# Layer 3's two store transfers issued by SP in place of ScalarE, placed between the loads of two steps

## The chip, the cores and the metric

The kernel runs on one core of a Trainium2 chip. A core has five engines that this text speaks of: TensorE (matrix products into PSUM), VectorE, ScalarE (activation functions), GpSimd, and SP, which here only issues transfers between the chip's main memory (DRAM) and on-chip memory (SBUF). Each engine works through its own list of instructions in order, and engines wait for one another by semaphores. The metric is the device time of one execution in microseconds (us), lower is better.

## The reference

The input is a float32 image tensor of 2 x 128 channels x 64 x 64. Four layers follow one another: layer 0 is a four-direction selective scan with layer norm and projections, layers 1 and 2 are spatial attention over 4096 positions, and layer 3, the one that is changed, is a short selective scan along the channels:

```python
seq = x.transpose(0, 2, 3, 1).reshape(B * H * W, TOKEN_NUM, D_MODEL)   # 8 tokens of 16
xz = seq @ in_proj_w.T;  xi, z = jnp.split(xz, 2, axis=-1)             # 32 inner channels
xs = jax.nn.silu(conv1d(xi))                                           # 4 taps, per channel
dt, Bm, Cm = jnp.split(xs @ x_proj_w.T, [1, 17], axis=-1)              # 16 states
dt = jax.nn.softplus(dt @ dt_proj_w.T + dt_proj_b)
h = exp(dt * A) * h + dt * Bm * xs                                     # 8 tokens in turn
y = (sum over states of h * Cm + xs * D) * silu(z)
out = y @ out_proj_w.T        # back to 128 channels; then group norm (4 groups), silu, + x
```

Every one of the 8192 pixels is a sequence of its own: its 128 channels are cut into 8 tokens of 16 channels. The recurrence over the tokens keeps 32 inner channels x 16 states per pixel.

## The kernel before, in words

In layer 3 a **chunk** is 512 pixels (T); there are 16 chunks, 8 for each of the two images. Within a chunk the 8 tokens are taken two at a time, so a chunk has four **steps** k = 0 to 3, and a step has two tokens, o = 0 and 1. The 128 partitions hold 4 state groups x 32 inner channels, and a tile of 4 x 512 elements per partition holds the other factor 4 of the states and the pixels. The arithmetic of a step uses four kinds of work:

- `spread(k)` (line 1232) loads the time step of two tokens from DRAM (`ddt`) into `dtr`, copied to the four partition groups: eight transfers of 64 KB, or four for k = 0. `da_(k)` (line 1273) is ScalarE's exponential of it, giving tile A.
- `load(k, o)` (line 1244) loads the 16 rows of B of one token from DRAM (`rows`) into a tile D, each row broadcast to 32 partitions: four transfers of 256 KB. A step has two such tiles, step 3 only one. There are six D buffers in turn, two `dtr` buffers.
- `db_` (line 1266) multiplies D, on VectorE and in two halves, by the time step times x (`rx`, from TensorE).
- The recurrence: `mul` (line 1283, GpSimd) multiplies A by the state before, `add` (line 1288, VectorE or GpSimd) adds that to D, which is then the new state. `hc_` (line 1306, VectorE) multiplies by C (`q`, from TensorE) and TensorE sums over the states into `y`.

`rows` and `ddt` are written once per chunk, one chunk ahead. `b_` makes B by a matrix product, ScalarE copies it from PSUM to SBUF (`bs`, line 1191), and the copy is stored to `rows` (line 1193). The time step `dt` is finished by GpSimd (`dt_add`, line 1217; `dtx_`, line 1220, makes dt times x), and is stored to `ddt` (line 1224). Both stores stand on ScalarE's list of instructions, all the loads on SP's.

The order of the instructions on each engine is written out by hand: the part runs under `manual_schedule`, and nothing is reordered. A loop over all steps s of all chunks has four groups g = 0 to 3 in a step. `PLAN` gives the recurrence of a group in letters: `m` is `mul` (on GpSimd), `v` and `g` are `add` on VectorE and GpSimd, `D` is `db_` for the step to come, `C` is `hc_` for the step before, `time` is `dt_add` and `dtx_`. For step 0, `PLAN` reads

```python
("m10 m11 C D", "C D time", "C v10 D", "g11 D C"),
```

and for step 1 `("m00 m01 C D v00", "C v01 D m10 m11", "v10 D", "g11 D")`. Other work is hung on a group by `more((k, g), ...)`, ahead of it (`at=first`) or behind it. The loads that go out in step s are those of step s + 2 (`n2`): in step 0 of a chunk the loads of its step 2, in step 2 those of the next chunk's step 0. The stores of the next chunk (`fut`) are in step 0: `b_` ahead of group 0, `put` behind group 2. The first chunk's own stores and loads stand ahead of the loop.

Each transfer signals its end on one of eight semaphores, which are given out in turn over the transfers of SP's and ScalarE's lists together, in an order set when the kernel is built. A transfer that gets a semaphore waits first until the transfer that had it before has landed.

Of the kernel before, what the change touches and what calls it, by code (L numbers as in the profile page):

```python
# [57 lines left out]
def conv_seq_kernel(ctx: ExitStack, tc: tile.TileContext, a: dict, out: bass.AP):  # L58
    nc = tc.nc
# [39 lines left out]
    with ExitStack() as c0:  # L99
# [9 lines left out]
        def wt(tag, bufs=None, shape=(P, 2, T)):  # L109
            return wk_.tile(list(shape), F32, tag=tag, name=tag, bufs=bufs)  # L110
# [386 lines left out]
        with tc.manual_schedule():  # L497
            c, c1 = chunks[:2]
# [234 lines left out]
    with ExitStack() as c1:  # L733
# [256 lines left out]
        def put(slot, *steps):  # L990
            for i, f in enumerate(steps):
                todo.setdefault(slot + i, []).append(f)

        def piece(slot, j, what, qd, later=0):

            steps = []

            def first():
                steps.extend(getattr(j, what)(qd))
                steps[0]()  # L1000

            n = 2 if j.layer == 2 else 7 if what == "value_piece" else 5
            put(slot, first, *[lambda i=i: steps[i]() for i in range(1, min(n, 5))])
            put(slot + 5 + later, *[lambda i=i: steps[i]() for i in range(5, n)])

        for n, j in enumerate(jobs):
            s0 = n * NG * UPG
            if n == 0:
                continue
            for g, what, qd in ((9, "key_piece", 0), (10, "value_piece", 0), (11, "key_piece", 1),  # L1010
                                (12, "value_piece", 1)):
                piece(s0 + (g - NG) * UPG + 5, j, what, qd)
            piece(s0 - UPG + 4, j, "key_piece", 2)
            piece(s0 - UPG + 9, j, "key_piece", 3)
            piece(s0 + 12, j, "value_piece", 2)
            piece(s0 + UPG + 2, j, "value_piece", 3)
            if jobs[n - 1].layer == 1:
                for ci in range(NCH):
                    c = Conv(jobs[n - 1].b, ci)
                    put(s0 + (1 + ci) * UPG + 11, lambda c=c: c.taps(0), lambda c=c: c.taps(1),  # L1020
                        lambda c=c: c.taps(2), c.end)
# [68 lines left out]
    with ExitStack() as c3:  # L1090
# [61 lines left out]
        class Chunk3:  # L1152
# [35 lines left out]
            def b_(self):  # L1188
                p = self.bc_(0)
                self.bs = wt("bs", (P, T), bufs=1)  # L1190
                nc.scalar.copy(self.bs, p)
                self.rows = dr.tile([P, T], F32, tag="rows", name="rows")
                nc.scalar.dma_start(self.rows, self.bs)

            def c_(self):
                self.pc = self.bc_(1)
# [24 lines left out]

            def put(self):
                self.ddt = dr.tile([P, 2, T], F32, tag="ddt", name="ddt")
                nc.scalar.dma_start(self.ddt, self.dt)

            def spread(self, k):

# [190 lines left out]
        with tc.manual_schedule():  # L1418
            mm(y, lhsT=ident, rhs=x[:, 0, 0:T], start=True, stop=True)
            c, c1 = chunks[:2]  # L1420
            for i in range(2):
                c.xs_(i)
            c.b_()
            for i in range(2):
                c.dt_(i)
            c.e_exp()
# [15 lines left out]
            for s in range(-1, len(steps) + 3):  # L1442
# [3 lines left out]
                fut = chunks[ci + 1] if s >= 0 and ci + 1 < len(chunks) else None  # L1446
# [8 lines left out]
                def more(key, *what, at=extra):  # L1455
                    at.setdefault(key, []).extend(what)

                if fut is not None:
                    more((0, 0), fut.b_, at=first)
                    more((0, 1), fut.c_, at=first)  # L1460
                    more((0, 2), fut.put, fut.cb_)
                if old is not None:
                    more((1, 0), lambda: old.yg_(1))
                    more((2, 1), old.xr_, at=first)
# [199 lines left out]
```

## Time and profile before

| | before |
|---|---|
| runs, us | 6688.31, 6689.05, 6681.28 (median 6688.31) |
| profiled execution, us | 6684.23 |
| its span, first to last instruction, us | 6682.4 |
| busy: TensorE, VectorE, ScalarE, GpSimd, us | 5857.7, 5536.6, 4477.6, 5404.5 |
| layer 3 (5640 to 6683): TensorE, VectorE, ScalarE, GpSimd, us | 846.61, 855.85, 473.99, 796.78 |
| granted TensorE clock, span and layer 3 | 0.863, 0.83 |
| store of rows, of ddt: issue on ScalarE's queue, us | 0.33, 0.33 |
| the same: issue to landing, us (median) | 2.0, 3.0 |
| load of D, of dtr: issue to landing, us (median) | 6.0, 3.0 |

The profile is of one execution. Engines are called PE (TensorE), PEld (its weight loads), DVE (VectorE), ACT (ScalarE), POOL (GpSimd) and SP; SPq and ACTq are the issues of transfers on an engine's list. A line of a list of waits reads: who waited, for what, the total in us, how many times, the longest. A line of the timeline reads: start and length in us, engine, line of the kernel, operation, output and inputs, count; in brackets the idle time of that engine just before it, and what ended that. What ended a wait is inferred from the semaphores.

### The profile page before, as it was taken

To read this page: it belongs to the slowest core of one execution; us is meant where nothing else is said; L and a number is where in the kernel's file an instruction comes from. 1 tells how busy PE (TensorE), PEld (TensorE's weight loads), DVE (VectorE), ACT (ScalarE), POOL (GpSimd) and SP (SyncE) were. 2 spreads that over 40 slices of the span, in tenths; PEclk is the share of its full clock that TensorE was granted. 3 is DMA by queue.
4 is the path that set the end of the run, shared out by engine and by line. 5 is a ranking of instruction groups with operands and counts; after the bars stand their busy time and mean duration, and the time that the engine had idled before them with its cause. 6 is when DMAs were issued, how large, how long until landed. Compare 5 with 4: busy or idle time off the path is not lost. (4 is left out here: it accounts for less than half of the span.)

```text
span 6682.4 us, 66184 instructions
## 1 busy us (share of the span) xinstructions
PE 5857.7 (88%) x19918; PEld 2766.3 (41%) x19918; DVE 5536.6 (83%) x4462; ACT 4477.6 (67%) x7740; POOL 5404.5 (81%) x2473
## 2 busy tenths in 40 slices
PE   8888888888888888888879999999999997888787
PEld 2222222222222222222228887787788885222221
DVE  7999999999999999999986665565566765788888
ACT  7887788877788777887766664455455554444443
POOL 6999999999999999999986665555556665788787
PEclk7888778877788778887779999999999998788888
DMA  6666666566656666665640000000000001766765
GB/s 182 145 155 157 156 149 150 147 150 152 151 143 146 154 154 148 154 149 146 146 106 5 4 4 1 1 1 1 1 1 1 1 1 26 198 160 163 187 162 138
DMA packets 400473, 700.59 MB, mean 105 GB/s; under 512 B 74089, under 2 KB 76530, under 8 KB 399730
## 3 DMA queue, kind: packets, MB, share of 16 engines
q1 hardware_dynamic: 394624, 681.74, 42.1%
q10 hardware_dynamic: 5490, 14.63, 0.6%
q8 instruction: 156, 2.56, 0.2%
q14 instruction: 203, 1.66, 0.1%
HBM read 584.80 MB, written 111.28 MB: 104 GB/s over the span
## 5 line engine op out<-in xcount | busy, mean ns | idle before, releaser
L384 POOL TENSOR_TENSOR dbu<-dus,bs 128x1024 f32<-128x1024 f32 x1024 | 2459.6, 2437 | 101.0 <-DVE h L428 86.5
L428 DVE TENSOR_TENSOR_SCAN h<-da,hst,dbu 128x1024 f32<-128x1024 f32 x896 | 2091.4, 2341 | 94.1 <-ACT dbu L412 88.8
L397 ACT ACTIVATE da<-dts,aneg 128x512 f32<-128x512 f32 (+1 forms) x2048 | 1410.2, 689 | 350.2 <-DVE h L428 312.1
L924 POOL TENSOR_TENSOR sum<-sum,sc 128x1024 f32<-128x1024 f32 x384 | 906.0, 2360 | 492.1 <-ACT sc L919 488.3
L886 ACT COPY sc<-s 128x512 f32<-128x512 f32 x1024 | 597.0, 584 | 859.7 <-PE s L881 745.8
L893 DVE TENSOR_TENSOR mx<-mx,s 128x512 f32<-128x512 f32 x896 | 609.4, 680 | 546.3 <-ACT sc L886 545.0
L881 PE MATMUL s<-q,k 128*128 128x256 f32 x4096 | 1051.8, 380 | 6.4 <-ACT q L838 3.0
L451 PE MATMUL y<-hc,cst 128*32 128x512 f32 x4096 | 881.8, 757 | 198.6 <-DVE hc L440 179.3
L936 PE MATMUL av<-sc,v 128*128 128x256 f32 x4096 | 1048.6, 379 | 2.5 <-ACT sc L919 2.5
L440 DVE TENSOR_TENSOR hc<-h,pc 128x1024 f32<-128x1024 f32 x704 | 842.1, 1196 | 10.7 <-PE y L451 8.6
L881 PEld LDWEIGHTS s<-q,k 128*128 128x128 f32 x4096 | 776.7, 190 | 140.5 <-issue 29.0
L936 PEld LDWEIGHTS av<-sc,v 128*128 128x128 f32 x4096 | 768.2, 190 | 102.9 <-ACT sc L919 3.9
L438 POOL TENSOR_TENSOR hc<-h,cs 128x1024 f32<-128x1024 f32 x320 | 761.2, 2379 | 1.1 <-issue 1.1
L417 PE MATMUL pc<-xd,sel 16*128 16x512 f32 x1024 | 707.9, 782 | 1.5 <-DVE hc L440 1.3
L1283 POOL TENSOR_TENSOR A<-A,D 128x1024 f32<-128x1024 f32 x224 | 526.8, 2370 | 194.1 <-DVE D L1288 146.4
L916 DVE TENSOR_TENSOR sc<-sc,pm 128x1024 f32<-128x1024 f32 x512 | 620.3, 1212 | 0.9 <-PE pm L912 0.9
L919 ACT ACTIVATE sc<-sc 128x1024 f32<-128x1024 f32 x512 | 542.0, 1059 | 8.6 <-DVE sc L916 8.1
L341 PE MATMUL misc<-xd,w_dt 9*128 9x512 f32 x504 | 371.6, 825 | 141.9 <-ACT x L480 78.3
L451 PEld LDWEIGHTS y<-hc,cst 128*32 128x32 f32 x4096 | 125.4, 120 | 855.7 <-DVE hc L440 419.2
L412 ACT ACTIVATE dbu<-hst,dbu,df 128x1 f32<-128x1 f32 x896 | 337.9, 377 | 81.6 <-POOL dbu L384 59.0
L1266 DVE TENSOR_TENSOR D<-D,rx 128x1024 f32<-128x1024 f32 x224 | 268.6, 1211 | 143.9 <-DMA D<-rows 120.3
L1300 PE MATMUL q<-xs,lc 32*128 32x512 f32 x896 | 301.0, 678 | 64.9 <-DVE A L1306 63.9
(263 smaller groups left out, 7561.9 us busy)
## 6 DMA issues: line engine op xcount, KB each, us to landing
dts<-ddt SPq DMA_DIRECT2D x512, 256.0 KB, 5.5
dus<-ddu SPq DMA_DIRECT2D x512, 256.0 KB, 5.0
D<-rows SPq DMA_DIRECT2D x448, 256.0 KB, 6.0
bs<-rows SPq DMA_DIRECT2D x1024, 64.0 KB, 4.9
cs<-rows SPq DMA_DIRECT2D x1024, 64.0 KB, 3.3
ddt<-dt SPq DMA_DIRECT2D x128, 256.0 KB, 2.0
ddu<-dtu SPq DMA_DIRECT2D x128, 256.0 KB, 4.0
dtr<-ddt SPq DMA_DIRECT2D x448, 64.0 KB, 3.0
```

Of the source, the lines that this page charges most:

```text
L384: nc.gpsimd.tensor_mul(t, self.dus[q], _bc(self.bs[g], 1, [P, 2, T]))
L397: act(t[:, i, sl], self.dts[q][:, i, sl], AF.Exp, scale=an[:, g, 2 * q + i : 2 * q + i + 1])
L417: mm(t, lhsT=sel[32:48, 4 * g : 4 * g + 4, :].rearrange("p n d -> p (n d)"), rhs=self.xd[32:48, :], start=True, stop=True)
L428: nc.vector.tensor_tensor_scan(ho, ai, bi, init, ALU.mult, ALU.add)
L438: nc.gpsimd.tensor_mul(t, self.h[u], _bc(self.cs[gq(u)[0]], 1, [P, 2, T]))
L440: nc.vector.tensor_mul(t, self.h[u], _bc(self.pc[u // 2], 1, [P, 2, T]))
L451: mm(self.y[q // 2][r : r + 32, :], lhsT=sum4, rhs=self.hc[u][:, i, :], start=False, stop=(u % 8 >= 6), skip_group_check=True)
L881: mm(p[:, o, :], lhsT=j.k[m // 8][:, m % 8 * P : m % 8 * P + P], rhs=self.q, start=True, stop=True)
L893: nc.vector.tensor_max(self.mx, self.s[0][:, 0:2, :] if u == 1 else self.mx, self.p[u])
L916: nc.vector.tensor_sub(s, s, _bc(self.pm[:, :], 1, [P, 4, NQ]))
L924: nc.gpsimd.tensor_add(self.sum, self.s[0] if w == 1 else self.sum, self.s[w])
L936: mm(self.av, lhsT=self.job.v[m // 8][:, m % 8, :], rhs=self.s[u // 2][:, m % 4, :], start=(m == 0), stop=(m == 31))
```

## The change

Both stores go to SP's list. The store of B becomes a method of its own, `put_b`. In the loop both are hung on group 3 of step 0, behind its arithmetic. On SP's list they then stand behind the loads that step 0 issues (those of step 2) and ahead of the loads that step 1 issues (those of step 3). ScalarE's copy `bs` and GpSimd's `dt_add` stay where they are on their engines. With the two transfers on one list, the eight semaphores are given out anew over layer 3.

```diff
                 nc.scalar.copy(self.bs, p)
                 self.rows = dr.tile([P, T], F32, tag="rows", name="rows")
-                nc.scalar.dma_start(self.rows, self.bs)
+
+            def put_b(self):
+                nc.sync.dma_start(self.rows, self.bs)
...
             def put(self):
                 self.ddt = dr.tile([P, 2, T], F32, tag="ddt", name="ddt")
-                nc.scalar.dma_start(self.ddt, self.dt)
+                nc.sync.dma_start(self.ddt, self.dt)
...
             c.b_()
+            c.put_b()
             for i in range(2):
                 c.dt_(i)
...
                     more((0, 0), fut.b_, at=first)
                     more((0, 1), fut.c_, at=first)
-                    more((0, 2), fut.put, fut.cb_)
+                    more((0, 2), fut.cb_)
+                    more((0, 3), fut.put_b, fut.put)
```

## The prediction, made before the changed kernel ran

> **What bounds the kernel now.** I began with the page: its chain of waits names transfers of D (D<-rows, 5% of the span) among the few large items that are no matmul. All of it lies in the last stretch, layer 3, so I asked for the busy times of that stretch.
>
> ```profile
> 5640.00:6683.00 1043.00, 846.61 (x2534) 217.74 (x2533) 855.85 (x700) 473.99 (x526) 796.78 (x324) 0.83 0.69 165
> ```
>
> Its columns are the length, then busy time of TensorE, its weight loads, VectorE, ScalarE and GpSimd, the granted clock, the DMA share and GB/s. VectorE is the fullest engine, 855.85 of 1043 us. What ends its idle time, over the same stretch:
>
> ```profile
> DVE D L1266 <- DMA D<-rows: 120.3, 22, 16.8
> DVE cb L1200 <- issue: 17.9, 1, 17.9
> DVE D L1266 <- PE q L1300: 16.6, 15, 1.9
> ```
>
> So one wait is nearly all of VectorE's loss: a copy of rows of B spread over the partitions (tile D) that has not landed. Listing VectorE's waits in time gives one large one per chunk, always at the first L1266 of step 1, 15 of them (4.34 to 7.70 us, 94.3 us together); the sixteenth chunk has none. Why is D late? The waits of SP's own queue, 5880 to 6640 us:
>
> ```profile
> SPq L1232 <- DMA rows<-bs: 188.7, 11, 20.7
> SPq L1232 <- DMA D<-rows: 88.9, 112, 1.5
> SPq L1232 <- ACT A L1273: 58.7, 16, 6.0
> ...
> SPq L1232 <- DMA ddt<-dt: 18.6, 10, 2.3
> ```
>
> L1232 loads dtr from ddt; it has no use for rows. Yet it waits for the store of rows once per chunk, 17 us on average. The instruction list of the built kernel says why: transfers of both queues take eight completion semaphores in turn, and each transfer first waits for the previous holder of its semaphore. In steady chunks the store of rows (on ScalarE's queue) holds the one that the first dtr load of step 2 takes next, and the store of ddt the one of the third. One chunk in the timeline:
>
> ```profile
> 6152.53 5.43 SPq L1244 DMA_DIRECT2D D<-rows  x8
> ...
> 6158.60 2.56 ACT L1273 ACTIVATE A<-dtr,aneg 128x512 f32<-128x512 f32 x4 [0.82 <-PE y L1316]
> ...
> 6163.89 9.35 POOL L1283 TENSOR_TENSOR A<-A,D 128x1024 f32<-128x1024 f32 x4 [1.16 <-DVE D L1288]
> ...
> 6173.30 0.33 ACTq L1193 DMA_DIRECT2D rows<-bs  x1
> ...
> 6175.39 5.67 SPq L1232 DMA_DIRECT2D dtr<-ddt  x8
> 6175.58 0.33 ACTq L1224 DMA_DIRECT2D ddt<-dt  x1
> ...
> 6181.17 3.68 SPq L1244 DMA_DIRECT2D D<-rows  x8
> ...
> 6188.83 1.22 DVE L1266 TENSOR_TENSOR D<-D,rx 128x1024 f32<-128x1024 f32 x1 [7.08 <-DMA D<-rows]
> 6189.97 1.22 DVE L1288 TENSOR_TENSOR D<-D,A 128x1024 f32<-128x1024 f32 x1
> ```
>
> SP stands still from 6157.96 to 6175.39, until the rows store has landed (2.0 us after its issue); then D of step 2 goes out at 6181.17 and VectorE, free at 6181.75, waits 7.08 us.
>
> **What the Trainium skill says.** "DMA: Bandwidth & Descriptors", section "Anatomy of one DMA", puts every semaphore wait on the issuing sequencer, before dispatch; so a blocked transfer blocks all behind it, as the 17 us above show. Its section "Issuing engines are not separate DMA queues" says transfers from any engine run on the same 16 DMA engines and a second issuer saves only issue time; that fits, since nothing here suggests the stores gain by ScalarE's queue, but no run yet shows the other placement. "SBUF — State Buffer", section "Who interferes with whom", calls the port shared by VectorE and GpSimd an exclusive lock. The trace agrees:
>
> ```profile
> 5891.68 2.35 POOL L1283 TENSOR_TENSOR A<-A,D 128x1024 f32<-128x1024 f32 x1 [1.30 <-DMA dtr<-ddt]
> ...
> 5892.65 2.46 DVE L1288 TENSOR_TENSOR D<-D,A 128x1024 f32<-128x1024 f32 x1
> ```
>
> GpSimd ends at 5894.03 and the add at 5895.11, 1.08 later; alone it takes 1.22.
>
> **The change part by part.** No engine's arithmetic changes, in number or order; 32 store issues move from ScalarE's queue to SP's.
>
> *Off ScalarE:* 32 issues of 0.33 us, 10.6 us over the layer, with waits for GpSimd. ScalarE is busy 474 of 1043 us and not waited for there; gain taken as 0 (ends: 0 to 5).
>
> *Onto SP:* two issues per chunk at the 0.43 us median of its D loads, 0.9 us; SP idles 17 us per chunk, so 0 (without that cover, 16 x 0.9 = 14 us).
>
> *The tie is cut.* In the changed list the order on SP is: dtr and D of step 2, rows, ddt, dtr and D of step 3; all semaphores now turn within one queue, so step 2's loads wait for no store. In the chunk shown, dtr can go when ScalarE has read its buffer, 6158.60 + 2.56 = 6161.2; eight issues (4.1 us, as that group took elsewhere) end at 6165.3, four of D(2,0) at 0.45 each at 6167.1. D(2,1) needs its buffer from GpSimd's second product, 6163.89 + 4.7 = 6168.6, and ends at 6170.4. D lands 6.0 us after issue (median; longest 9.8): D(2,0) at 6173 to 6177, before VectorE's 6181.75. This whole wait goes.
>
> *What is late next.* The multiply at 6181.75 ends at 6182.89, but the add behind it (6189.97 before) needs GpSimd's first product of step 1, and finds the second holding the port, until 6185.82. It ends at 6186.90 instead of 6191.19: 4.29 saved of 7.08. In other chunks GpSimd began that pair 2.9 us before VectorE was free and not 0.6; there, at 5946.45, VectorE was free at 5940.83, the pair ended at 5942.58, and the add ends at 5943.66 instead of 5948.81: 5.15 saved of 5.62. Done for each chunk from its own start of the pair:
>
> - five chunks of the first kind: 4.76 + 4.65 + 4.29 + 1.53 + 4.34 = 19.6
> - seven of the second: 5.15 + 5.63 + 5.07 + 5.41 + 5.67 + 4.94 + 5.32 = 37.2
> - the second and third chunk, where the tie also held the last load of D of step 1 (waits of 2.20 and 1.54 before the 7.13 and 5.89): 6.6 + 7.1 = 13.7
> - the first: SP is then held by its own loads (dtr behind D took 8.65 us at 5667.90); from 5681.8 the D loads would start at 5690.4, not 5692.69: 2.3 (ends 0 and 7.5)
>
> Sum 72.8 us.
>
> *The new wait:* SP stands at the stores for ScalarE's copy (6173.3) and GpSimd's dt_add (6175.6). Queued behind are dtr(3) and D(3,0), then the next chunk's first loads. dtr(3) anyway needs ScalarE's exponentials of step 1, done at 6179.5; with 3.6 and 1.8 us of issue D(3,0) is out at 6185.0 and lands at 6191 (6194.8 at the longest). VectorE wants it at 6201.72, or 6197.4 after the gain. Hidden, with 2.6 to 6.4 us to spare. The stores themselves leave when they do now; their readers come over 10 us later.
>
> Against its own time, span 6682.4 and 1.8 us around it: 6684.2 - 72.8 = 6611.4. The median of the runs, 6688.3, lies 4.1 above that execution: 6615.5, so 6616.
>
> **Rivals.**
> A. *The wait goes, but another takes part of it.* TensorE is busy 48.55 of a 59.90 us chunk and had caught up during the wait; with chunks near 55 us it is at 88%, and VectorE's 1.4 us wait for q may double or D's wait survive in part. For it: chunks had such a wait already, 15 of them. Against: in the chunk shown TensorE had the product for the next L1252 done by 6184.7 and the next q by 6185.8, and VectorE, saved or not, comes to them no earlier than 6187.6. At 2 to 3 us per chunk lost: 6616 + 30 to 45, about 6650.
> B. *Nothing moves:* D was late for its buffers or the DMA engines, not the tie. Against: SP's wait names rows, the engines are 69% busy, and the last chunk, with no stores, has no wait. 6688.
> C. *Slower:* the stores stop SP and D(3,0) comes late. That needs them to leave SP over 6.4 us later than now to cost anything, and over 10.7 us (6.4 + 4.3) to outweigh the gain; at 13 us, 2.3 us in each of 15 chunks, 6688 + 35 = 6723. Against: both producers' times are read off above, and neither depends on SP.
> D. *The full 94.3 us,* if GpSimd's pair shifts earlier too: 6594.
>
> **How the numbers follow.** Main case 0.62 (own range 6603 to 6630), A 0.25, D 0.05, B 0.04, C 0.04. Range 6594 to 6652: D, the main case and the nearer two thirds of A, 0.84, which takes in the unknown ends above. A tenth of a per cent separates the runs shown (6681 to 6689); 0.2% is 13 us, so faster is main, A and D: 0.92; same 0.04; slower 0.04.
>
> **What would show it.** SP's waits for rows by dtr gone; D of step 2 issued before the copy of bs ends, not 8 us after; VectorE's wait for D near 25 us (the start of the layer) instead of 120; the first add of step 1 long (2.5 to 3.4 us) where it was 1.22; chunks of 55 to 56 us. Wrong if the first L1266 of step 1 still waits for D, if another L1266 (steps 2, 3) begins to, or if waits for q grow by 2 us per chunk.

## The result, and the profile after

| | before | changed |
|---|---|---|
| median of the runs, us | 6688.68 (4 runs, 6681.28 to 6693.84) | 6625.15 (4 runs, 6620.86 to 6638.98) |
| changed to before, 95% interval | | 0.9909 [0.9892, 0.9927] |
| span of the profiled execution, us | 6682.4 | 6625.4 |
| layer 3: length, VectorE busy, VectorE idle, us | 1043, 855.85, 187.15 | 986, 871.74, 114.26 |

The changed kernel is 63.5 us faster by the medians, 57.0 us by the two profiled executions. The rest of this section explains the 57.0, since of these runs only those two have a trace.

In the changed kernel the lines of the methods below the stores are two further down: L1234 loads dtr, L1246 loads D, L1268 multiplies D, L1290 adds, L1308 multiplies by C; L1195 and L1226 are the two stores. First the busy times of layer 3, and of one chunk of 55.60 us (columns as in the prediction):

```profile
5640.00:6626.00 986.00, 838.69 (x2534) 213.65 (x2534) 871.74 (x700) 473.75 (x528) 795.07 (x324) 0.85 0.72 175
5949.70:6005.30 55.60, 50.44 (x158) 12.46 (x158) 53.91 (x43) 28.66 (x32) 49.34 (x21) 0.91 0.80 187
```

The layer is 57 us shorter with the same 700 instructions on VectorE. VectorE's idle time fell by 72.9 us, but its busy time rose by 15.9 us although it does the same work. In the steady chunk it is now busy 53.91 of 55.60 us, 97%. What ends its idle time, over layer 3:

```profile
DVE D L1268 <- DMA D<-rows: 28.2, 4, 16.4
DVE D L1268 <- PE q L1302: 22.2, 14, 3.0
DVE cb L1202 <- issue: 17.9, 1, 17.9
DVE A L1308 <- PE q L1302: 6.8, 6, 1.8
...
DVE y L1254 <- PE misc L1165: 6.7, 8, 1.3
DVE sz L1323 <- PE y L1318: 5.9, 4, 2.3
DVE D L1290 <- POOL A L1285: 4.0, 6, 0.7
```

The wait for D went from 120.3 us in 22 places to 28.2 in 4, and these four are all in the first chunk. The waits for TensorE grew: all lines of the list that name it add up to 29.3 us before and 44.0 after. The waits for GpSimd are 4.0 us, all of them of the add; before there was one of 0.2 us, and it was not the add's.

SP's own waits, 5800 to 6590 us, are of another kind:

```profile
SPq L1234 <- ACT A L1275: 207.0, 36, 10.7
SPq L1246 <- POOL A L1285: 52.2, 27, 4.0
SPq L1195 <- ACT bs L1191: 50.2, 11, 12.2
SPq L1246 <- DMA D<-rows: 33.3, 47, 1.1
...
SPq L1234 <- DMA D<-rows: 18.0, 27, 1.0
...
SPq L1226 <- POOL dt L1219: 10.0, 9, 1.9
```

The line "L1232 <- DMA rows<-bs" with its 188.7 us is gone but for a single wait of 0.2 us. SP now waits mostly for what a load really needs (a buffer that ScalarE or GpSimd has read), and at the stores for their producers. The waits for earlier transfers that remain are short: the longest of the 74 for loads of D is 1.1 us. One chunk in the timeline, and two lines of a later one:

```profile
5952.30 4.51 SPq L1234 DMA_DIRECT2D dtr<-ddt  x8
5956.95 5.18 SPq L1246 DMA_DIRECT2D D<-rows  x8
...
5965.85 0.59 ACT L1191 COPY bs<-misc 128x512 f32<-128x512 f32 x1 [5.06 <-PE misc L1184]
...
5966.46 0.34 SPq L1195 DMA_DIRECT2D rows<-bs  x1
...
5967.36 0.33 SPq L1226 DMA_DIRECT2D ddt<-dt  x1
...
5972.04 3.58 SPq L1234 DMA_DIRECT2D dtr<-ddt  x8
...
5973.05 4.71 POOL L1285 TENSOR_TENSOR A<-A,D 128x1024 f32<-128x1024 f32 x2
...
5975.90 1.21 DVE L1268 TENSOR_TENSOR D<-D,rx 128x1024 f32<-128x1024 f32 x1
...
5977.04 1.80 DVE L1290 TENSOR_TENSOR D<-D,A 128x1024 f32<-128x1024 f32 x1
...
6145.37 4.69 POOL L1285 TENSOR_TENSOR A<-A,D 128x1024 f32<-128x1024 f32 x2
...
6147.80 3.35 DVE L1290 TENSOR_TENSOR D<-D,A 128x1024 f32<-128x1024 f32 x1 [0.66 <-POOL A L1285]
```

D of step 2 starts to go out 8.9 us before ScalarE's copy `bs` begins; before the change it went 8 us after. The first L1268 of step 1 (5975.90) has no bracket: no wait. The add behind it takes 1.80 us and not 1.22: GpSimd's pair of products runs from 5973.05 to 5977.76, and the add ends at 5978.84, 1.08 us later, as in the example of the prediction. Where that pair is late, the add shows 3.35 us after a short wait, as in the last two lines, from another chunk.

Over the layer the adds on VectorE cost 276.8 us before (128 at a mean of 2162 ns) and 294.8 after (2303 ns):

```profile
L1288 DVE TENSOR_TENSOR D<-D,A 128x1024 f32<-128x1024 f32 x128 | 276.8, 2162 | 0.2
```

```profile
L1290 DVE TENSOR_TENSOR D<-D,A 128x1024 f32<-128x1024 f32 x128 | 294.8, 2303 | 4.7 <-POOL A L1285 4.0
```

So of the 92.1 us that the wait for D lost, 18.0 came back as longer adds, 3.8 as waits for GpSimd and 14.7 as waits for TensorE: 92.1 - 18.0 - 3.8 - 14.7 = 55.6, against 57.0 measured.

### The profile page after: what moved, and what is told of

Same layout as the page of the kernel before. It is cut to its first block, busy times and chain, and to the rows that moved or that the text cites. A ratio compares the mean times of both kernels' runs of the same rounds, so it can differ in the third digit from the quotient of the medians.

```text
span 6625.4 us, 66252 instructions
## 1 busy us (share of the span) xinstructions
PE 5849.6 (88%) x19918; PEld 2762.6 (42%) x19918; DVE 5553.3 (84%) x4462; ACT 4477.3 (68%) x7740; POOL 5402.6 (82%) x2473
## 5 line engine op out<-in xcount | busy, mean ns | idle before, releaser
L1302 PE MATMUL q<-xs,lc 32*128 32x512 f32 x896 | 306.7, 693 | 72.9 <-DVE A L1308 71.8
L417 PEld LDWEIGHTS pc<-xd,sel 16*128 16x128 f32 x1024 | 182.2, 218 | 352.3 <-issue 305.0
```

The lines of the kernel that those rows point to most:

```text
L417: mm(t, lhsT=sel[32:48, 4 * g : 4 * g + 4, :].rearrange("p n d -> p (n d)"), rhs=self.xd[32:48, :], start=True, stop=True)
```

## The experiments

Three questions were open: is the turn of the semaphores really the cause, and does it take both stores; is it the queue or the place in the order that matters; and what took back the part of the gain that did not show. The ratios below are to the kernel before, run beside each batch on the same chip. Beside the first three stood the changed kernel again, without an edit:

> The changed kernel again, for company to the next three on one chip. Both theories: 6620 to 6630, VectorE's wait for D near 28 us.

Measured: 6628.78 us, ratio 0.9913 [0.9895, 0.993], wait for D 28.6 us. It is as in the first result.

**One store alone.** The store of rows on SP in its new place, the store of ddt back on ScalarE in its old place:

```diff
-                nc.sync.dma_start(self.ddt, self.dt)
+                nc.scalar.dma_start(self.ddt, self.dt)
-                    more((0, 2), fut.cb_)
-                    more((0, 3), fut.put_b, fut.put)
+                    more((0, 2), fut.put, fut.cb_)
+                    more((0, 3), fut.put_b)
```

> Only the store of rows goes to SP behind the loads of step 0; the store of ddt stays on ScalarE's list where it was. In the built list ddt's semaphore is next taken by the third dtr load of step 2. Theory T (the tie through the semaphores' turn): SP still stands, now for ddt, until 3 us after its issue, the same moment at which the third dtr load went in the kernel before; D of step 2 comes as late as before, 6675 to 6690, VectorE's wait for D 90 to 120 us. Rival Q (it was the wait for rows alone, the longer one in the list, or the transfers on ScalarE's queue were slow): most of the gain, 6630 to 6645.

Measured: 6669.59 us, ratio 0.9982 [0.9976, 0.9989]. VectorE waits for D 113.4 us. The wait is as foretold, the time a little below the range. In the list of SP's waits the name in the tie has changed:

```profile
SPq L1234 <- DMA ddt<-dt: 205.9, 12, 21.2
```

Then the converse, ddt on SP and rows on ScalarE:

```diff
-                nc.sync.dma_start(self.rows, self.bs)
+                nc.scalar.dma_start(self.rows, self.bs)
-                    more((0, 0), fut.b_, at=first)
+                    more((0, 0), fut.b_, fut.put_b, at=first)
-                    more((0, 3), fut.put_b, fut.put)
+                    more((0, 3), fut.put)
```

> Only the store of ddt goes to SP behind the loads of step 0; the store of rows stays on ScalarE's list. Its semaphore is next taken by the second dtr load of step 2. Theory T: SP stands until rows has landed, some 3 us earlier than the third dtr load went before, so D of step 2 comes 2 to 3 us earlier: a third to a half of the gain, 6650 to 6670, VectorE's wait for D 60 to 90 us. Rival Q: nothing gained, 6685.

Measured: 6655.58 us, ratio 0.9953 [0.9934, 0.9972], wait for D 87.8 us. Again SP's loads of dtr wait for the store that stayed on the other list:

```profile
SPq L1234 <- DMA rows<-bs: 177.1, 12, 18.5
```

Either store left on ScalarE's list is enough to hold the loads: 205.9 and 177.1 us of waiting, for a store of the next chunk that these loads do not read. The gains of the two halves, 0.18% and 0.47%, add up to 0.65%, less than the 0.87% of both together in the same batch. That is what one tie that is enough would give, though the intervals don't keep the two sums firmly apart.

**The place without the queue.** Both stores in their new place of the order, but on ScalarE's list:

```diff
-                nc.sync.dma_start(self.rows, self.bs)
+                nc.scalar.dma_start(self.rows, self.bs)
-                nc.sync.dma_start(self.ddt, self.dt)
+                nc.scalar.dma_start(self.ddt, self.dt)
```

> The two stores at the place of the changed kernel (group 3 of step 0), but on ScalarE's list, where they then stand behind the four exponentials of step 1. Their semaphores are still next taken by the second and third dtr load of step 2. Theory T: SP stands for them and they leave 3 us later than before, so D of step 2 comes 3 us later: slower than before, 6710 to 6740, VectorE's wait for D 150 us or more. Rival P (the later place of the stores is what helped, the queue does not matter): 6625.

Measured: 6673.26 us, ratio 0.9984 [0.9977, 0.9991], wait for D 111.1 us. The loads still wait for the store:

```profile
SPq L1234 <- DMA rows<-bs: 202.6, 13, 19.8
```

The place alone is worth 0.16%, so the rest of the gain comes with the move to SP's list. But the expectation of a loss was wrong. It held that the stores, listed behind four exponentials (L1275), would leave after these. They left with the first of them:

```profile
6162.90 0.59 ACT L1191 COPY bs<-misc 128x512 f32<-128x512 f32 x1 [5.00 <-PE misc L1184]
...
6164.80 1.15 ACT L1275 ACTIVATE A<-dtr,aneg 128x1024 f32<-128x1024 f32 x1
6164.80 0.33 ACTq L1195 DMA_DIRECT2D rows<-bs  x1
6165.17 0.45 ACTq L1226 DMA_DIRECT2D ddt<-dt  x1
6165.85 3.21 ACT L1275 ACTIVATE A<-dtr,aneg 128x1024 f32<-128x1024 f32 x3
...
6166.84 3.92 SPq L1234 DMA_DIRECT2D dtr<-ddt  x7
```

ScalarE's list had handed out both transfers by 6165.62, while three of the four exponentials listed ahead of them had yet to start. In all fifteen chunks of the loop the store of rows left within 0.1 us of the start of the first exponential. So the store goes out 1.3 us after the copy `bs` has ended, where it was 0.04 us before the change, and the load that is tied to it is no later than that: SP's dtr goes out 2.0 us after the store, as it did before the change.

**The queue without the place.** The stores on SP's list, but rows ahead of the loads of step 0, at the place that it had on ScalarE's list:

```diff
-                    more((0, 0), fut.b_, at=first)
+                    more((0, 0), fut.b_, fut.put_b, at=first)
-                    more((0, 2), fut.cb_)
-                    more((0, 3), fut.put_b, fut.put)
+                    more((0, 2), fut.put, fut.cb_)
```

> Both stores on SP, but the store of rows ahead of step 0's loads (right behind the matrix product of B), the store of ddt behind them. Theory T (what matters is whether step 2's loads must wait for B's copy, by a semaphore's turn or by the order of the list): SP stands until the copy bs is done, but no longer until rows and ddt have landed; D of step 2 goes out 3 to 4 us earlier than before: about half of the gain, 6645 to 6665, VectorE's wait for D 60 to 85 us. Rival S (it is enough to have all transfers on one queue): 6620 to 6630.

Measured: 6631.93 us, but from 6621.2 to 6652.62, ratio 0.9934 [0.9912, 0.9956], wait for D 59.1 us. Now the loads stand behind the store itself, no semaphore is needed to hold them:

```profile
SPq L1195 <- ACT bs L1191: 204.4, 13, 22.1
```

```profile
6088.86 0.34 SPq L1195 DMA_DIRECT2D rows<-bs  x1
6089.25 5.46 SPq L1234 DMA_DIRECT2D dtr<-ddt  x8
```

The loads start right behind the issue of the store and not 2.0 us later, when it has landed; about half of the waiting for D goes by that alone. The expectation of 6645 to 6665 us was missed: the time lies next to that of its rival S, by which it is enough to have all transfers on one queue. The wait for D is 31 us longer than in the changed kernel, so the order behind the loads is better by the trace, by some 0.2% at the best estimate, but the intervals of the two ratios overlap and the times are not told apart. So by the best estimate the queue brings most of the gain; what the place behind the loads adds to it in time is not shown.

**Later still.** Both stores one step later, behind the loads of step 3 too:

```diff
-                    more((0, 3), fut.put_b, fut.put)
+                    more((1, 2), fut.put_b, fut.put)
```

> The changed kernel with the two stores moved once more, behind the loads of step 3 (group 2 of step 1). Theory H (the new stand at the stores is hidden): the same as the changed kernel within 0.2%, 6618 to 6632. Rival C (step 3's loads come late because of the stand): 6600 to 6612. Rival L (the stores were near their limit already): over 6640, with waits for D or dtr of the next chunk's step 0.

> Both stores one step later, behind the loads of step 3. If the stand of SP's list at the stores is hidden in the changed kernel: within 5 us of it, either sign. If that stand still costs something: 5 to 15 us below it, and the waits for D in the last step stay near 26 us.

Measured: 6611.19 us, ratio 0.9905 [0.9889, 0.9922], and in the last batch 6609.99 us, ratio 0.9896 [0.9878, 0.9914], where the changed kernel beside it had 6612.2. The first of the two fell into the range of rival C, since it had no changed kernel beside it; side by side the two can't be told apart. One step later SP no longer stands at the stores, but its loads of dtr for the next chunk then wait 81.3 us for the store of ddt, which they do read; no wait for D comes of it behind the first chunk. So the time that SP stands at the stores (50.2 and 10.0 us in the list above) is hidden in the changed kernel, as the prediction held, and the place one step later is as good, no better.

**What took the rest: the add in the way.** One try was to let the first add of step 1 go later, so that VectorE would not stand before GpSimd's port:

```diff
-            ("m00 m01 C D v00", "C v01 D m10 m11", "v10 D", "g11 D"),
+            ("m00 m01 C D", "C v00 v01 D m10 m11", "v10 D", "g11 D"),
```

> The changed kernel with the first add of step 1 put behind VectorE's product of group 1, next to the second add, so that work on PSUM stands where the add waited for GpSimd's pair. Theory K (the shared port): that add takes 1.2 us and not 2 to 3.4, VectorE's busy time in layer 3 falls by 10 to 20 us, and where GpSimd's pair is late the second add comes 2 us earlier: 6605 to 6618. Rival R (the chain through GpSimd decides: its third product now starts later): 6625 to 6645.

Measured: 6645.46 us, ratio 0.9952 [0.9933, 0.9971]: slower than the changed kernel, whose own interval lies just below in each batch. The timeline of one chunk shows where some of the time went:

```profile
6143.67 2.35 DVE L1290 TENSOR_TENSOR D<-D,A 128x1024 f32<-128x1024 f32 x2
6144.96 5.58 POOL L1285 TENSOR_TENSOR A<-A,D 128x1024 f32<-128x1024 f32 x2 [1.92 <-DVE D L1290]
...
6148.27 3.35 DVE L1290 TENSOR_TENSOR D<-D,A 128x1024 f32<-128x1024 f32 x1 [1.12 <-POOL A L1285]
```

The two adds are short now, 2.35 us together, but GpSimd's next products need the first one and wait 1.92 us for it, and then the next add waits and stands before GpSimd in its turn. Over the layer the adds cost 294.9 us, no less than in the changed kernel: the long add only moved. In addition VectorE's adds wait 17.9 us for GpSimd instead of 4.0, and line 1323 waits 19.4 us for TensorE's sum instead of 5.9, together 27.4 us more; the layer took 1003.6 us from its first copy `bs` on, against 979.6 in the first trace of the changed kernel. From the start of its pair of products to that of the next, GpSimd needs 6.61 us here (the pair began at 6138.35) where the changed kernel needed 5.86 (6145.37 to 6151.23). So in this chunk the long add is the cheaper of the two: it sits on a chain that goes VectorE, GpSimd, VectorE, and an early blocked add starts GpSimd sooner than a late free one.

**What took the rest: TensorE.** The waits for TensorE had grown by 14.7 us, which was the prediction's rival A. (The first expectation below compares 42 us with 24; the same lines counted on both sides are 41.6 and 27.5.) Two kernels give it less and more to do: one leaves out xs*D, one term of y, whose product is 64 of TensorE's instructions in the layer; the other halves D and makes this product twice, 64 more.

```diff
-                    more((1, 3), lambda: cc.y0_(0), at=first)
...
-                    more((3, 3), lambda: cc.y0_(1), at=first)
```

```diff
+        nc.vector.tensor_scalar(diag_d, diag_d, 0.5, None, ALU.mult)
...
-                mm(y, lhsT=diag_d, rhs=self.xs[:, i, :], start=False, stop=False,
-                   skip_group_check=True)
+                for _ in range(2):
+                    mm(y, lhsT=diag_d, rhs=self.xs[:, i, :], start=False, stop=False,
+                       skip_group_check=True)
```

The first alone, in the second batch:

> The changed kernel without the two products per chunk of xs with the diagonal of D (L1311; the term xs * D is left out of y). Theory A (of the 15 us missing from the forecast gain, TensorE took most: VectorE's waits for q, misc and y, 42 us against 24 before): those waits fall by 10 to 20 us and the time to 6605 to 6615. Rival K (the port that VectorE and GpSimd share took it): waits for q fall by less than 5 us, 6621 to 6630.

Measured: 6603.05 us, ratio 0.989 [0.9875, 0.9904]. That looked like a gain over the changed kernel, but the intervals overlap and the two were not in one batch. So all were measured again side by side:

> The changed kernel again, as the mark for the three that stand beside it: 0.990 to 0.993 of the kernel before, waits for D in the last step about 28 us.

> Leaves out the product xs*D of y, one 128x512 product of four a chunk and half on TensorE's queue; the output lacks that term. Theory TensorE (what did not come back of the waits for D is now waited for TensorE, which is near 90% busy in the shorter chunks): 10 to 20 us below the changed kernel. Rival (VectorE's own longer operations beside GpSimd and the chain through GpSimd set the rest): within 5 us of it.

> The opposite dose: D halved and its product with xs issued twice, so that TensorE has four more 128x512 products in a chunk and the result stays. Theory TensorE: 10 to 30 us above the changed kernel, with VectorE's waits for q, misc and y longer by about as much. Rival: within 5 us of it, the added products lie in TensorE's gaps.

| | median, us | ratio to before | VectorE's waits for q, us | its adds, us |
|---|---|---|---|---|
| changed kernel | 6612.2 | 0.9895 [0.9876, 0.9913] | 13.5 + 3.4 | 298.6 |
| without xs*D | 6611.64 | 0.9896 [0.9879, 0.9914] | 7.1 + 21.8 | 292.5 |
| xs*D twice | 6613.94 | 0.9896 [0.9878, 0.9914] | 36.7 + 4.9 | 285.7 |

Both medians are within 2 us of the changed kernel. But each ratio has an interval of 0.2%, some 12 us, and the theory foretold 10 to 20 us less and 10 to 30 us more: its upper part falls, its lower end does not. The first dose is no clean one either, since without xs*D TensorE was busy for 832.0 us of the layer, where the changed kernel's was for 824.1. The second added 16.6 us (840.7). The two lines that carry the reading are those of the adds, of the changed kernel in this batch and of the one with the product twice (there the line is one further down):

```profile
L1290 DVE TENSOR_TENSOR D<-D,A 128x1024 f32<-128x1024 f32 x128 | 298.6, 2333 | 6.0 <-POOL A L1285 5.2
```

```profile
L1291 DVE TENSOR_TENSOR D<-D,A 128x1024 f32<-128x1024 f32 x128 | 285.7, 2232 | 1.2 <-POOL A L1286 0.4
```

With more work on TensorE, VectorE waits 25 us longer for q, so the added products don't all lie in TensorE's gaps, as the rival had it. But its adds take 12.9 us less and wait 4.8 us less for GpSimd: it seems that a VectorE that comes later meets a GpSimd that has ended, and that about 18 of the 25 us only change their name. This is argued from one trace of each. The rest of the 25 us may well be real: from the first copy `bs` to the end, layer 3 took 977.9 us in the trace with the product twice and 967.4 in that of the changed kernel beside it, and the whole was no longer only because that copy came at 5634.32 and not at 5648.60, although the layers ahead have the same code. Yet without xs*D the layer took 976.4, so single traces don't settle a difference of 10 us. What these products cost, between nothing and some ten us, is open.

## Why the prediction was right

**The forecast.** It was 6616 us against 6688, a ratio of 0.9892. The first result is 0.9909 and the same kernel came to 0.9913 and 0.9895 later; faster was given 0.92. The mechanism was right and the size too large: 72.8 us of gain against 63.5 by the first medians, 54.5 in the first batch of experiments and 68.3 in the last. Some of the nearness is luck. The forecast is one of layer 3 and took the layers ahead as fixed, but in the traces of one and the same kernel they end up to 7.7 us apart. Layer 3 by itself, from its first copy `bs` to the end:

| trace | first `bs`, us | layer 3, us | VectorE's waits for TensorE, us | clock granted from 5640 on |
|---|---|---|---|---|
| before | 5644.46 | 1037.9 | 29.3 | 0.83 |
| changed kernel, first result | 5645.77 | 979.6 | 44.0 | 0.85 |
| the same, first batch | 5640.93 | 987.2 | 46.6 | 0.85 |
| the same, last batch | 5648.60 | 967.4 | 28.7 | 0.87 |

Against the one trace of before, the layer is 58.3, 50.8 and 70.5 us shorter.

**The tie is cut: right, and shown.** With either store left on ScalarE's list the loads wait for that store, and with both on SP's and behind the loads they wait for none (0.2 and 1.0 us remain). This is the one thing that the list of waits said and the diff did not. One direct test was not made: both stores on ScalarE's list with semaphores of their own. The Trainium skill's page "DMA: Bandwidth & Descriptors", section "Anatomy of one DMA", which is written of the transfers that GpSimd issues, has a semaphore wait hold the issuing sequencer; SP's waits of 205.9, 177.1 and 202.6 us, each with the loads of D standing behind it, show the same on SP's list.

**The saved wait is not all saved: right.** The prediction's sum of 72.8 takes 98.0 us of waits (the 94.3, and 2.20 and 1.54 of two chunks more), leaves 5.4 of them to the first chunk and gives 19.9 back to GpSimd's late pair and the port. So 92.6 us of waiting were to go, and 92.1 us of the wait for D went. Measured on the other side: 18.0 us of longer adds and 3.8 of waits for GpSimd, 21.8 together. The section "Who interferes with whom" of "SBUF — State Buffer" calls the port an exclusive lock; the add of 3.35 us that ends at 6151.15, 1.09 after GpSimd's pair, is what that looks like in the trace.

**The waits for TensorE: the step that was mis-sized.** The prediction put rival A wholly on another branch and gave it nothing in its main sum, since in the chunk that it worked out TensorE was ahead. In the first trace these waits grew by 14.7 us, about 1 us per chunk, half of the 2 to 3 us that rival A priced. The 15.8 us between 72.8 and 57.0 are this term and 1.9 us more at the port, nearly. The chunk shown above took 55.60 us, as foretold, but on average from one copy of `bs` to the next it is 57.8 us (808.7 us over 14) instead of 61.7: 3.9 us less, where the prediction's sum makes 5.0. The term is not a fixed cost. In the trace of the last batch the waits for TensorE are 28.7 us, no more than before the change, and there the layer is 70.5 us shorter, close to the forecast. In the table above, and in the two traces with the stores one step later (0.86 and 34.7, 0.86 and 35.8), a higher granted clock goes with shorter waits; that it is the cause was not tested. Whether the term can be bought back by giving TensorE less to do was not shown either way.

What bounds the steady chunk now is VectorE: busy 97% of the chunk shown, 94% of the 14 (756.70 of 808.70 us). But that busy time is not all its own work. An add that meets nobody takes 1.22 us and the 128 adds have a mean of 2.30, so by estimate some 139 us of the adds' 294.8 are time before the port that GpSimd holds.

**SP at the stores: hidden, right.** Behind the first chunk nothing waits for D, and moving the stores away from there again changed nothing. *Off ScalarE* and *the two issues on SP*, both put at nothing, can't be seen in any run.

**The first chunk.** It was given 2.3 us; its wait of 7.70 us became 3.31 and, at another multiply of D, 2.98: 1.4 less in all. So two signs of being wrong did show, in this one chunk of sixteen: the first multiply of step 1 still waits, and another began to.

**The other rivals.** A (another engine takes part of the wait) came true in part, as above. B (nothing moves) and C (slower) fell with the result, D (the full 94.3 us) with the long adds. The signs named were found in the other chunks: dtr's wait for rows gone, D of step 2 out ahead of `bs`, 28.2 us of waiting for D (25 foretold), long first adds.

## What to carry to other kernels

When a list of transfers waits for one that the waiting load has no use for, look at how the kernel gives out its completion semaphores. Here eight of them went in turn over two issuing lists, and one store left on the other list was enough to hold the loads; it took both stores on the loads' own list to cut the tie, and a place behind the loads so that the order of the list does not hold them instead. Price the removed wait by what stands behind it and comes due next (here GpSimd's pair of products and the port), then add a term for every engine that had been catching up during it, TensorE here. And when the engine that waited is nearly always busy afterwards, ask how much of that busy time it spends before a port that another engine holds.

## What the runs showed of the hardware that was not expected

- ScalarE's list issues transfers ahead of activations listed before them: in the chunk shown both stores were out 0.8 us after the start of the first of four exponentials, of which three had not begun. A place "behind" an activation on that list does not delay a store until the activation has run.
- TensorE's products don't have one duration. In the changed kernel a pair of 128x512 products (line 1311) took 2.08 us at 6017.49, and a pair took 1.02 at 5983.16. In both traces of the kernel with 64 products fewer the granted clock of the layer was lower (0.81 and 0.82) than in the others with the order of the changed kernel (0.85 to 0.87), and in that of the last batch TensorE was busy for 832.0 us where the changed kernel's was for 824.1, so that the work taken from it did not come back as free time there. In the other trace without these products it was busy for 806.9 us. What sets the clock and the durations is open.
